# A four-layer convolution and attention kernel: residual statistics from known means, an output loop in three stages, and layer 2's statistics by sums and squares, for the last image

## The chip, the cores and the metric

The kernel runs on one core of a Trainium2 chip. The metric is the device time of one execution in microseconds (us); a kernel's time is the median of its runs. Beside those runs one execution was taken by the hardware profiler, and all lines of profile come from that one. Engines are called as in the profile: PE (TensorE, matrix products), PEld (its weight loads), DVE (VectorE), ACT (ScalarE), POOL (GpSimd) and SP (SyncE, which here only issues transfers). Each works through its own queue in order.

## The reference

Four images of 256 channels by 64 x 64 pixels, fp32. Four layers follow each other; each normalises its input by groups of 8 channels and adds its result to it.

```
x = x + L0(gn(x))   # 3x3 conv, group norm, relu -> xs; attention over the 4096 pixels; 0.1 * group_norm(w . y) + xs
x = x + L1(gn(x))   # linear attention: qkv of the rms-normed input, softmaxes, context, w_out, rms norm
x = x + L2(gn(x))   # a 3x3 depth-wise filter and a 256x256 point-wise one, both generated from the pooled input
x = x + L3(gn(x))   # one 256x256 matrix, mixed from four by a gate on the pooled input
```

`gn(x)` needs the mean and the variance of every channel of the layer's input. So between two layers lies a point where all pixels of an image must have been written and counted before the next layer can begin.

## The kernel before, in words

An image is held as two halves of 128 channels (`h`), each 128 partitions by 4096 pixels. Line 1448 on is the order of the whole: the convolution of image 0, its projections, and then, for each image, its attention (`attend`, line 887) side by side with everything else there is to do: the tail (layers 0's residual, 1, 2 and 3) of the image before and the convolution of the image after. `run` (line 1424) takes one step of a `Chain` and one step of the attention by turns. A step of the attention is eight matmul instructions of 512 columns on PE (logits, L895, and the product with the values, L934), two exponentials on ACT (L896) and one sum on DVE. All engines' queues are filled in this written order; nothing reorders them later. A `Chain` (line 45) turns the yields of its layers into steps: a yield of 0.6 at rate 1 is 0.6 of a step. `later(n, f)` emits `f` after n steps.

The last image has no attention of a next image to run beside its tail. Its tail (`tail` with `diag`, `xs_in` and `held`, line 1387) therefore runs alone at the end, with these differences:

- Layer 3's products of the image before it are held back (`held`, 16 pieces, line 1371): `fill(n)` emits n of them as work for PE at places where PE would wait, and `settle()` emits the additions on DVE and the output transfers on SP that belong to them.
- `nonlocal_out` (line 948) is layer 0's residual: for each of eight parts of 1024 columns, `big = wy * sc + xs` on DVE (through `stt`, L127), then two `bn_stats` of 512 columns each (L984). `group_finish` (line 330) joins such statistics with `bn_aggr`, averages over a group by a small matmul, and takes the inverse root with POOL. For the last image `xs` is `x_cols`, loaded into the core before its tail begins.
- `linear_attention` (line 990) ends in an output loop over eight units of 512 pixels: `outputs` (L1092 products, L1094 Squares with accumulator on ACT, then maximum on DVE and inverse root on POOL), `scaled` (the products times that root, two of four blocks on ACT at L1105 and two in one DVE operation), and `added` for the unit before (transposes on PE at L1115, addition on DVE, `bn_stats` at L1117).
- `generated` (line 1139) is layer 2: a pooled hidden layer (L1169), normalised input into `xp`, the filter `dk`, then eight parts of 1024 columns. Five of these take their taps on DVE (`taps`, eight `stt` each, L127, from ACT's `centre`, L1211), three on PE with diagonal matrices (`taps_by_products`, L1254, copied out by ACT at L1257). The point-wise matrix `pk` is summed on DVE from eight slices (`load_wp2`, loaded by SP). `pointwise` (L1219) multiplies, and `pointwise_added` adds to `big` and counts with `bn_stats` (L1228).
- `mixed` (line 1304) is layer 3: gate, a weighted sum of four matrices on DVE (L1334 and L127), scaled for each half (L1343), a bias from a small product (L1348), then 16 products (L1357), each with an addition and an output transfer.

PSUM has eight banks of 512 columns, given out in turn by `bank`; `k4` and `k2` are pools of nine tiles of 1024 and five tiles of 512 columns.

Of the kernel before, what the change touches and what calls it, by code (L numbers as in the profile page):

```python
# [13 lines left out]
P = 128  # L14
NH = 2
# [78 lines left out]
def conv_preact_fast(ctx: ExitStack, tc: tile.TileContext, guard, x, wc, wtpg, ww, wqkv, wout, w1cat, wd2,  # L94
# [235 lines left out]
    def group_finish(st, avg, eps, shift=None):  # L330


        mv = sp.tile([P, NH, 2], F32, name="mv")
        for h in range(NH):
            nc.vector.bn_aggr(mv[:, h, :], st[:, h, :, :].rearrange("p c s -> p (c s)"))
# [614 lines left out]


    def nonlocal_out(w, b, big, k4, xs_in):
# [19 lines left out]
        _, gm, rstd = yield from group_finish(wy_stats[b], avg32, 1e-5, bias)  # L972
        sc, sh = affine(gm, rstd, vec_s[:, V_G2W, :], vec_s[:, V_G2B, :], bias, 0.1)
        st = stats_tile()
        w.fill(2)
        for i, (c, h) in enumerate(PARTS):
# [6 lines left out]
            for s in range(2):  # L983
                nc.vector.bn_stats(st[:, h, 2 * c + s, :], big[:, h, bass.ts(2 * c + s, 512)])  # L984
# [5 lines left out]
    def linear_attention(w, b, big, qT, k4, st, sh, alone):  # L990
# [95 lines left out]
        def outputs(c):  # L1086
            zr = sp.tile([P, 4], F32, name="zr", bufs=3)
            banks = []
            for s in range(2):
# [5 lines left out]
                banks.append(ps)  # L1095
            nc.vector.tensor_scalar(zr, zr, 1e-24, None, ALU.max)
            rsqrt(zr, zr)
            return zr, banks

        def scaled(zr, banks):  # L1100
            z = k4("z").rearrange("p (j o) -> p j o", j=4)
            for s in range(2):
                if alone and s == 0:
                    for j in range(2):
                        nc.scalar.activation(z[:, j, :], banks[0][:, j, :], AF.Copy, scale=zr[:, j:j + 1])  # L1105
                    continue
                tt(z[:, bass.ts(s, 2), :], banks[s], zr[:, bass.ts(s, 2)].unsqueeze(2).to_broadcast([P, 2, NH * P]), ALU.mult)
            return z

        def added(c, z):  # L1110
            cols = bass.ts(c, 512)
            for h in range(NH):
# [5 lines left out]

        last = None
        for c in range(NC):  # L1120
            zb = outputs(c)
            yield 0.6
# [9 lines left out]
        w.fill(2)  # L1132
# [5 lines left out]
    def generated(w, b, big, k4, st, sh, diag):  # L1138
        _, gm, rstd = yield from group_finish(st, avg8, 1e-5, sh)
# [4 lines left out]
        w1n = sp.tile([P, NH, HP], F32, name="w1n")  # L1144
# [58 lines left out]
        st = stats_tile()  # L1203
# [20 lines left out]
        def pointwise_added(c, res):  # L1224
            cols = bass.ts(c, 512)
            for oh in range(NH):
                tt(big[:, oh, cols], res[oh], big[:, oh, cols], ALU.add)
                nc.vector.bn_stats(st[:, oh, c, :], big[:, oh, cols])  # L1228
# [36 lines left out]
        w.settle()  # L1265
# [4 lines left out]
        for n, i in enumerate(mine):  # L1270
# [9 lines left out]
            if n == 0:  # L1280
                for j in range(R):
# [19 lines left out]
    def mixed(w, b, big, k4, st, sh, held):  # L1301
# [29 lines left out]
        wm = k2("wm")  # L1331
        for j in range(NE):
            if j == 0:
                nc.vector.tensor_scalar(wm, ex[j // 2][:, j % 2, :], al[:, 0:1], None, ALU.mult)  # L1334
            else:
                stt(wm, ex[j // 2][:, j % 2, :], al[:, j:j + 1], wm, ALU.mult, ALU.add)
            yield 0.5

        mix = wm.rearrange("p (h o) -> p h o", h=NH)
        wm = []  # L1340
        for h in range(NH):
            wm.append(mix[:, h, :] if held is None else filter_tile("wmh")[:, 0, :])
            nc.vector.tensor_scalar(wm[h], mix[:, h, :], rstd[:, h:h + 1], None, ALU.mult)  # L1343
        yield 1
        pb3 = bank("ps_b3")
        for oh in range(NH):
            for h in range(NH):
                nc.tensor.matmul(pb3[:, oh:oh + 1], wm[h][:, bass.ts(oh, P)], off[:, h:h + 1],  # L1348
                                 start=(h == 0), stop=(h == NH - 1))
        b3 = sp.tile([P, NH], F32, name="b3")  # L1350
        tt(b3, sh, pb3[:, 0:NH], ALU.subtract)

        def product(c, oh):
            cols = bass.ts(c, 512)
            ps = bank("ps_ex")
            for h in range(NH):
                nc.tensor.matmul(ps, wm[h][:, bass.ts(oh, P)], big[:, h, cols], start=(h == 0), stop=(h == NH - 1))  # L1357

            def added():
                res = k2("res")  # L1360
# [3 lines left out]

        w.settle()
        for c in range(N // 512):
            for oh in range(NH):
# [659 lines left out]
```

## Time and profile before

| | |
|---|---|
| runs | 3123.15, 3116.27, 3117.10 us; median 3117.1 |
| the profiled execution: its own time, its span | 3122.35, 3120.6 us |
| busy PE, DVE, ACT, POOL | 3005.0, 2129.1, 1138.5, 131.1 us of the span |
| attention, 1024 exponentials of 128x512 on ACT (L896) | 603.7 us, 597 ns each |
| attention, 2048 + 2048 matmul instructions (L895, L934) | 968.8 and 962.1 us |
| the last eight matmul instructions of the last attention start | 2813.1 us |
| last image's tail: residual from | 2829 us |
| its layer 1: first product, first product of the output loop | 2855.4, 2922.7 us |
| its layer 2: first product of the hidden layer, first point-wise product | 2973.4, 3004.4 us |
| its layer 3: first product | 3085.6 us |

How to read it: a line of a timeline is start, duration, engine, line, operation, the tiles written and read, shapes, and how often; in brackets the idle time of the engine before it and what ended that. A line of the chain is start, duration and what the end waited for in that stretch. Matmuls overlap, so the duration of one (592 ns for 512 columns) is longer than the distance between two of them (430 ns). A matmul in fp32 appears as two instructions.

### The profile page before, as it was taken

The numbers are of one execution on the slowest core, as the hardware profiler recorded it, in microseconds if no ns is written. First come the engines' busy times: TensorE is split into PE (matmuls) and PEld (weight loads), VectorE is DVE, ScalarE is ACT, GpSimd is POOL, SyncE is SP. The second block draws the span as 40 slices with busy tenths as digits, with TensorE's granted clock in tenths as the row PEclk, the third lists the DMA queues.
The fourth block names the chain that finished last, engine by engine and source line by source line (L and its number), as shares of the span: only waits on it lengthen the run. The fifth ranks groups of instructions, "written<-read, shape, count | busy, mean of one in ns | idle before, by whom it ended". The sixth has DMA issues, their size and how long they took to land.

```text
span 3120.6 us, 24280 instructions
## 1 busy us (share of the span) xinstructions
PE 3005.0 (96%) x8606; PEld 1487.8 (48%) x8606; DVE 2129.1 (68%) x2700; ACT 1138.5 (36%) x2100; POOL 131.1 (4%) x178
## 2 busy tenths in 40 slices
PE   6899999999999999999999999999999999996888
PEld 3354555445554444444565444444555544443533
DVE  8747777853557986786537896878353768855485
ACT  2134333353545332223454432322355453333510
POOL 0100000000110000000001000000000100000100
PEclk9999999999999999999999999999999999998999
DMA  5233111032001023113200102310510010120011
GB/s 217 80 101 136 37 48 35 26 59 88 33 11 34 7 74 125 41 44 81 88 11 1 41 29 86 104 41 24 128 48 1 11 41 7 47 74 34 14 61 65
DMA packets 58912, 174.25 MB, mean 56 GB/s; under 512 B 6432, under 2 KB 16416, under 8 KB 54560
## 3 DMA queue, kind: packets, MB, share of 16 engines
q1 hardware_dynamic: 54752, 155.85, 14.5%
q0 software_dynamic: 4032, 16.78, 2.9%
q8 instruction: 70, 1.15, 0.1%
q14 instruction: 58, 0.48, 0.0%
HBM read 111.26 MB, written 78.12 MB: 61 GB/s over the span
## 4 chain that ended last, share of the span: by engine, by line
PE 76%; DVE 17%; issue 5%; ACT 1%; POOL 0%; DMA 0%; POOLq 0%; ACTq 0%; DVEq 0%
PE pf L895 22%; PE py L934 22%; PE ps_qkv L1024 5%; PE ps_conv L496 4%; DVE dw L127 4%; PE ps_tp L871 4%; PE ps_ex L1357 3%; DVE tot L124 3%; PE ps_pw L1219 3%; PE ps_conv L568 2%; PE ps_g L876 2%; PE ps_wy L918 1%; PE ps_o L1092 1%; DVE big L127 1%; PE ps_ctx L1046 1%
## 5 line engine op out<-in xcount | busy, mean ns | idle before, releaser
L896 ACT ACTIVATE pr<-pf 128x512 f32<-128x512 f32 x1024 | 603.7, 597 | 1194.1 <-PE pf L895 1148.6
L895 PE MATMUL pf<-tpg 128*128 128x512 f32 x2048 | 968.8, 595 | 1.5 <-ACT pr L896 1.5
L934 PE MATMUL py<-pr,tpg 128*128 128x512 f32 x2048 | 962.1, 592 | 3.0 <-ACT pr L896 2.9
L124 DVE TENSOR_TENSOR tot<-tot,pr 128x1024 f32<-128x1024 f32 x448 | 546.4, 1220 | 182.6 <-ACT pr L896 181.3
L934 PEld LDWEIGHTS py<-pr,tpg 128*128 128x128 f32 x2048 | 388.9, 190 | 494.7 <-issue 478.3
L895 PEld LDWEIGHTS pf<-tpg 128*128 128x128 f32 x2048 | 382.0, 190 | 436.1 <-issue 411.4
L127 DVE SCALAR_TENSOR_TENSOR dw<-xp,dk,dw 128x1008 f32<-128x1008 f32 x216 | 273.0, 1268 | 6.8 <-ACT dw L1211 3.7
L496 PE MATMUL ps_conv<-v,u 128*128 128x512 f32 x384 | 170.8, 592 | 0.0
L1024 PE MATMUL ps_qkv<-wqkv_s,xg 128*128 128x384 f32 x384 | 129.9, 487 | 0.0
L124 DVE TENSOR_TENSOR tpg<-ps_g,bg_s 128x512 f32<-128x512 f32 x32 | 22.1, 692 | 145.6 <-PE ps_g L876 145.6
L871 PE MATMUL ps_tp<-big,wtpg_s 128*128 128x512 f32 x256 | 118.1, 605 | 3.0 <-ACT big L668 3.0
L496 PEld LDWEIGHTS ps_conv<-v,u 128*128 128x128 f32 x384 | 72.8, 190 | 92.2 <-issue 91.2
L217 POOL TENSOR_TENSOR rstd<-rstd,half 128x2 f32<-128x2 f32 x24 | 16.8, 700 | 2375.5 <-DVE rstd L351 2181.1
L1219 PE MATMUL ps_pw<-dw,pk 128*128 128x512 f32 x224 | 104.6, 601 | 8.1 <-DVE dw L127 8.1
L909 DVE RECIPROCAL inv<-pss 128x512 f32<-128x512 f32 x32 | 107.3, 3352 | 7.1 <-PE pss L907 7.1
L1024 PEld LDWEIGHTS ps_qkv<-wqkv_s,xg 128*128 128x128 f32 x384 | 72.2, 190 | 53.6 <-issue 9.3
L1034 DVE TENSOR_REDUCE qs<-qk 128x16 f32<-128x512 f32 x24 | 16.5, 686 | 118.6 <-ACT qk L1028 118.6
L872 ACT ACTIVATE tpg<-ps_tp,btp_s 128x512 f32<-128x512 f32 x64 | 43.8, 687 | 119.6 <-PE ps_tp L871 119.6
L871 PEld LDWEIGHTS ps_tp<-big,wtpg_s 128*128 128x128 f32 x256 | 47.9, 195 | 55.0 <-issue 50.6
L1094 ACT ACTIVATE junk<-ps_o 128x256 f32<-128x256 f32 x128 | 49.2, 384 | 67.5 <-PE ps_o L1092 59.4
L1219 PEld LDWEIGHTS ps_pw<-dw,pk 128*128 128x128 f32 x224 | 43.0, 192 | 62.6 <-issue 52.0
L1028 ACT ACTIVATE qk<-ps_qkv,rinv 128x256 f32<-128x256 f32 x96 | 45.6, 475 | 72.4 <-PE ps_qkv L1024 61.6
(309 smaller groups left out, 3120.7 us busy)
## 6 DMA issues: line engine op xcount, KB each, us to landing
xp<-in_x_dram SPq DMA_DIRECT2D x16, 1024.0 KB, 6.3
wy_d<-wt SPq DMA_DIRECT2D x32, 512.0 KB, 3.0
out_dram<-res SPq DMA_DIRECT2D x64, 256.0 KB, 2.0
wy<-wy_d SPq DMA_DIRECT2D x28, 512.0 KB, 4.7
xs_d<-big POOLq DMA_DIRECT2D x24, 512.0 KB, 11.0
u<-filters SPq DMA_DIRECT2D x48, 256.0 KB, 2.5
xs<-xs_d SPq DMA_DIRECT2D x24, 512.0 KB, 5.3
u<-rows_d SPq DMA_DIRECT2D x36, 256.0 KB, 3.1
```

Source lines behind the costliest of these rows:

```text
L124: nc.vector.tensor_tensor(o, a, b, op)
L127: nc.vector.scalar_tensor_tensor(o, a, s, b, op0, op1)
L496: nc.tensor.matmul(ps[oh], u(oh, h), v[:, bass.ts(h, 512)], start=(h == 0), stop=(h == NH - 1))
L568: nc.tensor.matmul(ps[:, bass.ts(oh, IY * IX)], u[i][:, h, bass.ts(oh, P)], v[:, i, bass.ts(h, IY * IX)], start=(h == 0), stop=(h == NH - 1))
L871: nc.tensor.matmul(ps, wtpg_s[:, h, k, :], big[:, h, cols], start=(h == 0), stop=(h == NH - 1))
L895: nc.tensor.matmul(pf, phi[:, bass.ts(2 * m + s, P)], theta[:, bass.ts(q, 512)], start=True, stop=True)
L896: nc.scalar.activation(pr[:, bass.ts(s, 512)], pf, AF.Exp)
L909: nc.vector.reciprocal(inv, pss)
L934: nc.tensor.matmul(py, g[:, bass.ts(2 * m + s, P)], probs[i][:, bass.ts(s, 512)], start=(m == 0 and s == 0), stop=(m == NM - 1 and s == 1))
L1024: nc.tensor.matmul(ps[:, 0:3 * HID], xg[:, h, bass.ts(j, P)], wqkv_s[:, h, :], start=(h == 0), stop=(h == NH - 1))
L1219: nc.tensor.matmul(ps, pk[:, h * NH * P + oh * P:h * NH * P + (oh + 1) * P], dw[h][:, bass.ts(s, 512)], start=(h == 0), stop=(h == NH - 1))
L1357: nc.tensor.matmul(ps, wm[h][:, bass.ts(oh, P)], big[:, h, cols], start=(h == 0), stop=(h == NH - 1))
```

## The change

It concerns the last image's tail above all; `mixed`, the place of a `settle` and a small operation (`pivot`) in `generated` change for all images.

- Sums of the last image's `xs` are taken on ACT (Copy with accumulator, 16 times 512 columns) during the last steps of the last attention, three for each step. The mean of the residual is then known before it is written: the mean of `wy` (from the statistics that the attention has taken) times `sc`, plus the mean of `xs`. After each update of 1024 columns ACT takes the Square about this mean with an accumulator, in place of two `bn_stats` on DVE.
- The output loop of layer 1 (`alone`) emits the next unit's products ahead of the scaling of this one and the addition of the one before. The inverse root of the next unit is emitted between the two halves of the addition. Three of four blocks are scaled on ACT and one on DVE.
- In layer 2, for the last image, `big` is written with an accumulator (sum) on DVE, and ACT takes a Square about a pivot with an accumulator; `st()` makes mean and variance of them. `settle`, which stood before the taps, stands after the first part's taps.
- In layer 3 the matrices are mixed half by half with the normalisation's scale already in the gate; the first four products are emitted first half by first half, with the bias matmul between the halves.

```diff
-        mv = sp.tile([P, NH, 2], F32, name="mv")
-        for h in range(NH):
-            nc.vector.bn_aggr(mv[:, h, :], st[:, h, :, :].rearrange("p c s -> p (c s)"))
+        if callable(st):
+            mv = st()
+        else:
+            mv = sp.tile([P, NH, 2], F32, name="mv")
+            for h in range(NH):
+                nc.vector.bn_aggr(mv[:, h, :], st[:, h, :, :].rearrange("p c s -> p (c s)"))
...
+    res_sum = cp.tile([P, NH], F32, name="res_sum")
+    def residual_sums(xs_in):
+        parts = sp.tile([P, NH, N // 512], F32, name="res_parts", bufs=1)
+        for h in range(NH):
+            for c in range(N // 512):
+                nc.scalar.activation(junk(), xs_in[:, h, bass.ts(c, 512)], AF.Copy, accum_out=parts[:, h, c:c + 1])
+                yield
+        nc.vector.tensor_reduce(res_sum, parts, AX.X, ALU.add)
...
+        wmv, gm, rstd = yield from group_finish(wy_stats[b], avg32, 1e-5, bias)
         sc, sh = affine(gm, rstd, vec_s[:, V_G2W, :], vec_s[:, V_G2B, :], bias, 0.1)
         st = stats_tile()
+        if xs_in is not None:
+            mv = sp.tile([P, NH, 2], F32, name="mv_in", bufs=1)
+            centre = sp.tile([P, NH], F32, name="centre", bufs=1)
+            squares = sp.tile([P, NH, N // CH], F32, name="squares", bufs=1)
+            tt(mv[:, :, 0], wmv[:, :, 0], bias, ALU.subtract)
+            tt(mv[:, :, 0], mv[:, :, 0], sc, ALU.mult)
+            stt(mv[:, :, 0], res_sum, 1.0 / N, mv[:, :, 0], ALU.mult, ALU.add)
+            nc.vector.tensor_scalar(centre, mv[:, :, 0], -1.0, None, ALU.mult)
+            def moments():
+                nc.vector.tensor_reduce(mv[:, :, 1], squares, AX.X, ALU.add)
+                nc.vector.tensor_scalar(mv[:, :, 1], mv[:, :, 1], 1.0 / N, None, ALU.mult)
+                return mv
+            st = moments
         w.fill(2)
...
             yield 0.6
-            for s in range(2):
-                nc.vector.bn_stats(st[:, h, 2 * c + s, :], big[:, h, bass.ts(2 * c + s, 512)])
+            if xs_in is not None:
+                nc.scalar.activation(wy, big[:, h, cols], AF.Square, bias=centre[:, h:h + 1], accum_out=squares[:, h, c:c + 1])
+            else:
+                for s in range(2):
+                    nc.vector.bn_stats(st[:, h, 2 * c + s, :], big[:, h, bass.ts(2 * c + s, 512)])
             yield 0.6
         w.settle()
...
+            return zr, banks
+        def root(zr):
             nc.vector.tensor_scalar(zr, zr, 1e-24, None, ALU.max)
             rsqrt(zr, zr)
-            return zr, banks
         def scaled(zr, banks):
             z = k4("z").rearrange("p (j o) -> p j o", j=4)
+            if alone:
+                for j in range(4):
+                    src = banks[j // 2][:, j % 2, :]
+                    if j < 3:
+                        nc.scalar.activation(z[:, j, :], src, AF.Copy, scale=zr[:, j:j + 1])
+                    else:
+                        nc.vector.tensor_scalar(z[:, j, :], src, zr[:, j:j + 1], None, ALU.mult)
+                return z
...
-        def added(c, z):
+        def added(c, z, halves=range(NH)):
             cols = bass.ts(c, 512)
-            for h in range(NH):
+            for h in halves:
...
+        if alone:
+            this, last = outputs(0), None
+            root(this[0])
+            for c in range(NC):
+                after = outputs(c + 1) if c + 1 < NC else None
+                z = scaled(*this)
+                for h in range(NH):
+                    if last is not None:
+                        added(c - 1, last, (h,))
+                    if h == 0 and after is not None:
+                        root(after[0])
+                this, last = after, z
+                w.settle()
+                if c in (2, 4):
+                    w.fill(1)
+                yield 1
+            added(NC - 1, last)
+            w.fill(2)
+            return st
...
-        w.fill(2)
...
+        mv, gm, rstd = yield from group_finish(st, avg8, 1e-5, sh)
+        pivot = sp.tile([P, NH], F32, name="pivot")
+        tt(pivot, sh, mv[:, :, 0], ALU.subtract)
...
-        st = stats_tile()
+        if diag is None:
+            st = stats_tile()
+        else:
+            sums = sp.tile([P, 2, NH, N // 512], F32, name="sums", bufs=1)
+            def st():
+                both = sp.tile([P, 2, NH], F32, name="both_m", bufs=1)
+                mv = sp.tile([P, NH, 2], F32, name="mv")
+                nc.vector.tensor_reduce(both, sums, AX.X, ALU.add)
+                nc.vector.tensor_scalar(both, both, 1.0 / N, None, ALU.mult)
+                tt(pivot, pivot, both[:, 0, :], ALU.add)
+                tt(pivot, pivot, pivot, ALU.mult)
+                tt(mv[:, :, 1], both[:, 1, :], pivot, ALU.subtract)
+                nc.vector.tensor_copy(mv[:, :, 0], both[:, 0, :])
+                return mv
...
             for oh in range(NH):
-                tt(big[:, oh, cols], res[oh], big[:, oh, cols], ALU.add)
-                nc.vector.bn_stats(st[:, oh, c, :], big[:, oh, cols])
+                if diag is None:
+                    tt(big[:, oh, cols], res[oh], big[:, oh, cols], ALU.add)
+                    nc.vector.bn_stats(st[:, oh, c, :], big[:, oh, cols])
+                else:
+                    nc.vector.scalar_tensor_tensor(big[:, oh, cols], res[oh], 1.0, big[:, oh, cols], ALU.mult, ALU.add,
+                                                   accum_out=sums[:, 0, oh, c:c + 1])
+                    nc.scalar.activation(junk(), big[:, oh, cols], AF.Square, bias=pivot[:, oh:oh + 1],
+                                         accum_out=sums[:, 1, oh, c:c + 1])
...
         dw = {mine[0]: centre(mine[0])}
-        w.settle()
...
             if n == 0:
+                w.settle()
                 for j in range(R):
...
-        wm = k2("wm")
-        for j in range(NE):
-            if j == 0:
-                nc.vector.tensor_scalar(wm, ex[j // 2][:, j % 2, :], al[:, 0:1], None, ALU.mult)
-            else:
-                stt(wm, ex[j // 2][:, j % 2, :], al[:, j:j + 1], wm, ALU.mult, ALU.add)
-            yield 0.5
...
+        scales = sp.tile([P, NH, NE], F32, name="scales")
+        for h in range(NH):
+            nc.vector.tensor_scalar(scales[:, h, :], al, rstd[:, h:h + 1], None, ALU.mult)
+        mix = k2("wm").rearrange("p (h o) -> p h o", h=NH)
         wm = []
         for h in range(NH):
             wm.append(mix[:, h, :] if held is None else filter_tile("wmh")[:, 0, :])
-            nc.vector.tensor_scalar(wm[h], mix[:, h, :], rstd[:, h:h + 1], None, ALU.mult)
-        yield 1
-        pb3 = bank("ps_b3")
-        for oh in range(NH):
-            for h in range(NH):
-                nc.tensor.matmul(pb3[:, oh:oh + 1], wm[h][:, bass.ts(oh, P)], off[:, h:h + 1],
-                                 start=(h == 0), stop=(h == NH - 1))
+            for j in range(NE):
+                e = ex[j // 2].rearrange("p k (h o) -> p k h o", h=NH)[:, j % 2, h, :]
+                if j == 0:
+                    nc.vector.tensor_scalar(wm[h], e, scales[:, h, 0:1], None, ALU.mult)
+                else:
+                    stt(wm[h], e, scales[:, h, j:j + 1], wm[h], ALU.mult, ALU.add)
+                if j % 2 == 1:
+                    yield 0.6
+        yield 0.5
...
+        def bias():
+            pb3 = bank("ps_b3")
+            for oh in range(NH):
+                for h in range(NH):
+                    nc.tensor.matmul(pb3[:, oh:oh + 1], wm[h][:, bass.ts(oh, P)], off[:, h:h + 1],
+                                     start=(h == 0), stop=(h == NH - 1))
+            tt(b3, sh, pb3[:, 0:NH], ALU.subtract)
+        def multiply(ps, c, oh, h):
+            nc.tensor.matmul(ps, wm[h][:, bass.ts(oh, P)], big[:, h, bass.ts(c, 512)], start=(h == 0), stop=(h == NH - 1))
...
+        pieces = [(c, oh) for c in range(N // 512) for oh in range(NH)]
+        if held is not None:
+            bias()
+            for c, oh in pieces:
+                held.append(lambda c=c, oh=oh: lambda added=product(c, oh): added()())
+            return
...
         w.settle()
-        for c in range(N // 512):
-            for oh in range(NH):
-                if held is not None:
-                    held.append(lambda c=c, oh=oh: lambda added=product(c, oh): added()())
-                else:
-                    w.later(1, product(c, oh)())
-                    yield 0.1
+        first = [bank("ps_ex") for _ in range(4)]
+        for h in range(NH):
+            for ps, (c, oh) in zip(first, pieces):
+                multiply(ps, c, oh, h)
+            if h == 0:
+                bias()
+        for ps, (c, oh) in zip(first, pieces):
+            w.later(1, adder(ps, c, oh)())
+            yield 0.1
+        for c, oh in pieces[4:]:
+            w.later(1, product(c, oh)())
+            yield 0.1
...
+        sums = residual_sums(x_cols)
         while next(attention, False):
+            for _ in range(3):
+                next(sums, None)
+        for _ in sums:
             pass
         next(last)
```

Left out: `w1n` gets one buffer in place of two; where the loop for the other images called `outputs`, it now calls `root` right after it; `product` and `adder` are the former `product` in two parts.

## The prediction

> **What bounds the kernel now.** I read the page's chain first, then the chain in order of time for the last image, then busy time by stage, then the waits and the engines' timelines there.
>
> ```profile
> PE 76%; DVE 17%; issue 5%; ACT 1%; POOL 0%; DMA 0%; POOLq 0%; ACTq 0%; DVEq 0%
> ```
>
> TensorE (PE) sets the end for most of the span: until 2816 us the attention keeps it at 20.00 of 20 us. Only the last image's tail, 2816 to 3120, has holes. Busy time by stage (columns: length, then PE, PEld, DVE, ACT, POOL, the clock, DMA):
>
> ```profile
> 2820.00:2840.00 20.00, 7.07 (x18) 2.64 (x16) 17.40 (x35) 1.89 (x4) 0.70 (x1) 0.88 0.29 105
> 2840.00:2860.00 20.00, 5.75 (x17) 4.23 (x18) 13.09 (x26) 5.04 (x6) 0.76 (x2) 0.50 0.07 26
> 2940.00:2960.00 20.00, 15.83 (x72) 11.12 (x70) 15.15 (x28) 11.34 (x44) 4.03 (x4) 0.91 0.12 40
> 3020.00:3040.00 20.00, 20.00 (x48) 8.93 (x47) 18.74 (x20) 1.64 (x2) 0.00 (x0) 1.00 0.00 0
> 3040.00:3060.00 20.00, 20.00 (x48) 8.93 (x47) 18.94 (x22) 1.17 (x2) 0.00 (x0) 1.00 0.00 0
> ```
>
> The residual (first two rows) is VectorE's (DVE) alone, with ScalarE (ACT) idle. Layer 1's output loop (third) fills no engine. Layer 2's taps (last two) fill DVE and PE, PE without a gap. The chain in the residual, then the waits in the loop (total, times, longest):
>
> ```profile
> 2829.07 1.29 DVE tpg L127
> ...
> 2846.71 1.19 DVE tpg L127
> 2847.92 1.29 DVE st L984 x2
> 2849.21 1.31 DVE res L127 x2
> ```
>
> ```profile
> DVE zr L1096 <- ACT junk L1094: 12.3, 6, 3.3
> PEld ps_zt L1115 <- ACT z L1105: 5.9, 8, 1.8
> ACT junk L1094 <- issue: 5.1, 2, 2.6
> ```
>
> Every update of 1024 columns is followed by two statistics, 2.5 us a part. In the loop each engine waits for the one before it: a latency ring, not a full engine. Then three places of the tail, from the timelines:
>
> ```profile
> 2964.75 5.46 PE L1357 MATMUL ps_ex<-big,wmh 128*128 128x512 f32 x8
> ```
>
> ```profile
> 2985.94 0.75 DVE L127 SCALAR_TENSOR_TENSOR res<-ps_ex,b,big 128x512 f32<-128x512 f32 x1 [0.97 <-PE ps_ex L1357]
> ```
>
> ```profile
> 3013.60 2.07 PE L1219 MATMUL ps_pw<-dw,pk 128*128 128x512 f32 x2 [8.14 <-DVE dw L127]
> ```
>
> Held-back products delay the statistics' matmul (the next one, at 2970.0); held-back sums on DVE stand before the first tap; PE waits 8.14 us for the second part's taps, and from there to 3070.7 the chain is PE in one piece.
>
> **The skill.** *ScalarE: Activation LUTs*, section "What ACT_TABLE_LOAD costs": an ACTIVATE with a bias pointer takes 280 ns + 0.833 ns an element, and neighbours overlap by some 93 ns. For 1024 columns that is 1.13; the trace has 1.15 (L1211, one pointer) and 1.06 (L1002, Square, none): it agrees. Reading the accumulator is a second instruction of 0.19 (L1094). *TensorE: Matmul & The Clock Gate*, Part 1: after about 3.4 us of idling PE runs at half rate until it has been busy as long. The trace agrees: six point-wise matmuls took 5.49 us after the 8.14 us wait, eight take 3.43 later.
>
> **The change part by part.**
>
> A, the residual. Before, from the first update (2829.07) to the mean's shift (2851.06): 22.0 us. After: four small operations at 0.20 apart (as 2826.22, .41, .61), 0.8; eight updates at 1.28 (row of 128x1024), 10.2; then ACT's last Square, 1.15 + 0.19 + a semaphore, 1.4, beside the two held-back sums of 1.39 on DVE; a reduction and a scaling, 0.4. Sum 12.8, so **-9.2**. ACT's Squares (1.15 - 0.09 + 0.19 = 1.25 a part) hide behind the updates. If ACT can't overlap (1.44 a part) the gain is 8.0; with updates at 1.20, as the chain has some, 9.8. The last two parts' data, asked for at 2827 and landing after 4 to 5 us, are wanted at 2837.
>
> The new input sums run under attention: 16 Copies with accumulator at some 0.54 + 0.22 = 0.76, three a step: 2.3 beside 1.2 of exponentials in a 3.43 us step, just full. Behind them in ACT's queue stand the next exponentials, which PE wants 1.7 us later; the excess of 0.05 a step is covered. The tail before ends at 2787, and 5.4 of the 7 steps left are needed. Cost 0; 2 if not covered.
>
> B, the output loop. Before, from the weights (2922.69) to the group mean's copy (2970.36): 47.7. After: first Squares done at +3.2, the next unit's four (0.505 each) at +5.2, three scalings (0.37 apart) at +6.3, transposes: DVE begins at +7.1. Then its own work bounds: 16 adds with statistics at 1.385, 22.2; six scalings of 256 columns at 0.34, 2.0; six maxima, 0.6; two held-back sums, 1.4: 26.2, to +33.3. ACT needs 4 x 0.505 + 3 x 0.37 = 3.1 a unit against DVE's 3.25, PE 2.6. Two fills of 1.72 on PE stand before the next unit's products and cost about 0.5 each over PE's slack: +34.4. Aggregation and first group matmul: 1.4, so +35.8, **-11.9**. The moved root step is one DVE maximum (0.1, between the two adds) and GpSimd's power of 1.01, on a queue that holds nothing else here; its result is wanted one unit later, 3 us on, so it leaves the path. The third scaling goes from DVE to ACT, which is why DVE's share drops from 0.6 to 0.34. The last eight held-back matmuls start at about +30 and end at +33.7, before the statistics: their stall is gone. If fills stay at half clock as before (3.3 and 5.5 us) I get +39.2, -8.5; with no waits -13.2.
>
> C, the sums moved behind the first taps. Taps wait for the filter (2981.76) and ACT's centre (ends 2982.94): start at 2983.0 for 2986.6, -3.6. The four sums now follow the taps: 4 x 0.68 = +2.7. But SyncE (SP) queues their four output DMAs ahead of the third and fourth load of wp2 (before: all issued 2987.1 to 2988.6). Taps end 2993.3, sums 2996.0; the load is issued at 2996.4 and lands after 3.3 to 7.1, median 4.5, at 3000.9; DVE wants it after four products of 0.78, at 2999.1: +1.8. Net **+0.9** (-0.3 to +3.5). This moves PE's start at 3013.6 one for one.
>
> D, layer 2's statistics. DVE loses 16 x 0.6 us, but PE is full from 3013.6: nothing. At the end, instead of bn_stats 0.69 and aggregation 0.59: accumulator read 0.08, Square on 512 columns 0.77, six small operations 1.17: **+0.75** (0.5 to 1.1). A wait is added: ACT's Square waits for DVE's add, and behind it stand the copies of the PE-made depth-wise parts, which PE reads 2.8 us later at the tightest (3063.8 against 3067) and about 7 and more elsewhere: covered.
>
> E, weights in halves: before, four operations of 512 columns and two of 256 end on DVE at 3082.5; after, two tiny ones and eight of 256 (0.31 to 0.43) end at about the same time, the first half 1.7 earlier. But PE works on twelve held-back matmuls from 3077.9 to 3084.9 either way, and the bias matmuls (0.8) only change places: 0. With those twelve gone, the half would be worth its 1.7.
>
> The other images get the new order and a pivot operation of 0.16, which on every image lies in the 0.7 that DVE waits for GpSimd's power. PE is full there: 0, with -1 to +2 kept for four banks held at once.
>
> Sum: -9.2 - 11.9 + 0.9 + 0.75 = -19.5. The profiled execution took 3122.35 (span 3120.6 and 1.7 around it): 3102.9. It lies 5.25 over the runs' median of 3117.1, inside their spread; for the median, **3097.6**.
>
> **Rivals.**
> - *PE falls to half clock in the whole new loop.* Then PE needs 5.3 a unit and sets the pace; the loop comes to about 54 instead of 47.7: B is +7, total near -1, 3116. For: both fills ran at half clock before. Against: the other products ran full at half PE's load; now its share is 2.6 of 3.3. Chance 0.06.
> - *More comes free:* fills at full clock, no wait for wp2, the cold start at 3013 shortened: -25, 3092. For: the 3 us cold penalty there. Against: the 8 us wait stays. 0.12.
> - *The input sums come late*, after attention, since the tail before takes longer: 12 us of ACT before the last eviction: 3110. Against: 7 steps are left. 0.05.
> - *Slower:* the new Squares hold the depth-wise copies back. If each of six copies keeps PE waiting by two taps (2.6) and one window at half rate (1.7), 26 us are lost: +6.3, 3123. It decides once a copy is over 2.8 us late, every time; DVE, relieved of 10 us, should run ahead. 0.06.
>
> **Numbers.** Forecast 0.68; the remaining 0.03 within noise. A measurement of this kernel can tell about 0.2%, 6.2 us, from no change. Faster: 0.68 + 0.12 and half of the late sums, 0.83; same 0.11; slower 0.06. The unknown costs' bounds give 3093 to 3108; with the runs' spread 3090 to 3109.
>
> **What would show it.** Right: updates 1.28 apart in the residual and Squares beside them on ACT; 3.3 to 3.5 us a unit in the loop; the first tap 1.3 us after the filter; a wait of DVE for wp2; PE in one piece after its first point-wise matmul; the twelve held-back matmuls still ahead of the last products. Wrong: PE gaps in the taps, half clock in the loop, attention steps over 3.43 us near its end.

## The result and the profile after

The kernel after takes 3114.51 us (median of 20 runs, 3113.49 to 3116.23) against 3119.19 for the kernel before in the same sets (20 runs): a ratio of 0.9982 [0.9976, 0.9988], 4.7 us less where 19.5 were forecast. A second set on one chip gave 3114.24 (21 runs) against 3119.99 (36 runs), 0.9978 [0.9972, 0.9985]. The runs of before lie in two groups, near 3117 and near 3123, and its profiled execution (3122.35) belongs to the upper one; so the two profiles differ by 8.8 us of span (3120.6 and 3111.8), which is what the stages below add up to, and the medians by less. The later experiments are compared with 3114.24; the profile of that second set is called the second profile of after.

The stages of the two profiles, from marks in their timelines (us; the first mark of before is 2812.89 there, not 2813.1 as in the table ahead of the prediction):

| stage | before | after | difference | forecast |
|---|---|---|---|---|
| start of the span to the start of the last attention's last eight products | 2812.89 | 2816.68 | +3.8 | 0 |
| to the copy of the group mean behind the residual (A) | 39.01 | 29.07 | -9.9 | -9.2 |
| to the group mean behind layer 1 (its attention and B) | 118.46 | 114.62 | -3.8 | -11.9 |
| to PE's first point-wise product on taps made by DVE (C) | 43.24 | 47.13 | +3.9 | +0.9 |
| to the end of the last point-wise product (D's stretch) | 57.13 | 54.10 | -3.0 | 0 |
| to the group mean behind layer 2 (D's end) | 2.76 | 3.41 | +0.65 | +0.75 |
| to the end (E) | 47.1 | 46.8 | -0.3 | 0 |

The page's chain has the same shares as before, so it can't tell where the time went; it is a view of the whole span, and the tail is a tenth of it:

```profile
PE 76%; DVE 17%; issue 5%; ACT 1%; DMA 0%; POOL 0%; POOLq 0%; SPq 0%; DVEq 0%; ACTq 0%
```

Busy time by stage (length, then PE, PEld, DVE, ACT, POOL, the clock as the share of PE's full rate that was granted, DMA share and GB/s):

```profile
2820.00:2840.00 20.00, 13.98 (x27) 5.63 (x25) 16.06 (x32) 6.89 (x13) 0.70 (x1) 0.83 0.30 105
2840.00:2860.00 20.00, 11.84 (x34) 7.79 (x34) 7.52 (x18) 12.19 (x21) 1.76 (x3) 0.57 0.07 27
2920.00:2940.00 20.00, 17.41 (x77) 11.30 (x76) 11.32 (x23) 15.11 (x57) 5.04 (x5) 1.00 0.00 1
3020.00:3040.00 20.00, 20.00 (x48) 8.93 (x47) 16.35 (x20) 5.03 (x12) 0.00 (x0) 1.00 0.00 0
3040.00:3060.00 20.00, 20.00 (x48) 8.93 (x47) 11.38 (x19) 6.06 (x14) 0.00 (x0) 1.00 0.00 0
```

In the residual (first two rows) ACT now works beside DVE. In the output loop (third row) the clock is full, so PE did not fall to half rate there. DVE is busy for only 11.3 of 20 us, so it does not set the pace, as the forecast had said it would. In layer 2 (last rows) DVE is relieved and PE is as full as before.

**The residual** went as forecast. Its chain, and one pair of instructions of ACT from the timeline:

```profile
2834.89 8.45 DVE tpg L127 x7
...
2843.34 1.32 DVE res L127 x2
```

```profile
2843.37 1.15 ACT L1014 ACTIVATE wy<-tpg,centre 128x1024 f32<-128x1024 f32 x1
2844.43 0.19 ACT L1014 ACTIVATION_READ_ACCUMULATOR wy<-tpg,centre 128x1 f32 x1
```

Seven updates follow each other every 1.2 us with nothing between, and the last Square (1.15 + 0.19) ends 2.6 us after the last update began.

**The output loop** has a new ring. The timeline of one unit, cut to its links:

```profile
2933.00 1.01 POOL L217 TENSOR_TENSOR zr<-zr,half 128x4 f32<-128x4 f32 x1 [3.45 <-DVE zr L1132]
...
2934.04 1.20 ACT L1141 ACTIVATE z<-ps_o,zr 128x256 f32<-128x256 f32 x3 [1.36 <-POOL zr L217]
...
2935.35 0.48 DVE L1143 TENSOR_SCALAR z<-ps_o,zr 128x256 f32<-128x256 f32 x1 [1.14 <-ACT z L1141]
...
2935.75 0.74 DVE L127 SCALAR_TENSOR_TENSOR tpg<-ps_zt,gains,tpg 128x512 f32<-128x512 f32 x1
...
2936.53 0.69 DVE L1156 BATCH_NORM_STATS2 st<-tpg 128x6 f32<-128x512 f32 x1
...
2937.14 0.15 DVE L1132 TENSOR_SCALAR zr<-zr 128x4 f32<-128x4 f32 x1
...
2937.46 1.01 POOL L217 TENSOR_TENSOR zr<-zr,half 128x4 f32<-128x4 f32 x1 [3.45 <-DVE zr L1132]
```

Read the starts: POOL's root (1.04), ACT's three scalings (1.31), DVE's scaling (0.40), the addition (0.78), its statistics (0.61), the maximum (0.32), and POOL again: 4.46 us. The line to look at is the third: DVE scales block 4, which POOL's root has made ready at 2934.01, but begins only when ACT has finished blocks 1 to 3. It reads another part of `ps_o` and writes another part of `z`; what it shares with ACT is the PSUM bank of blocks 3 and 4. The semaphores in the trace say that this instruction waits for ACT and POOL; DVE's scaling in the kernel before, of a bank of its own, waited for POOL alone.

**Upstream**, in the other images, PE waits where it had not (total, times, longest), and the timeline shows the place:

```profile
PE ps_conv L499 <- DVE v L124: 3.6, 2, 1.8
```

```profile
1252.04 3.70 PE L499 MATMUL ps_conv<-v,u 128*128 128x512 f32 x8 [1.78 <-DVE v L124]
```

**The wait for wp2** is there, and longer than forecast:

```profile
2993.99 3.11 DVE L127 SCALAR_TENSOR_TENSOR pk<-wp,pb,pk 128x512 f32<-128x512 f32 x4 [3.29 <-DMA wp<-in_wp_dram]
```

```profile
2985.73 2.31 SPq L1450 DMA_DIRECT2D out_dram<-res  x4
2988.13 0.91 SPq L1223 DMA_DIRECT2D wp<-in_wp_dram  x2
```

SP issued the four output transfers first; the load went out at 2988.13 and landed 5.77 us later, after which DVE could go on.

### The profile page after: what moved, and what is told of

It reads as the page before. It is cut to its first block, busy times and chain, and to the rows that moved or that the text cites. A ratio compares the mean times of both kernels' runs of the same rounds, so it can differ in the third digit from the quotient of the medians.

```text
span 3111.8 us, 24418 instructions
## 1 busy us (share of the span) xinstructions
PE 3006.8 (97%) x8606; PEld 1486.8 (48%) x8606; DVE 2109.5 (68%) x2713; ACT 1174.0 (38%) x2188; POOL 131.1 (4%) x178
## 3 DMA queue, kind: packets, MB, share of 16 engines
q8 instruction: 70, 1.15, 0.2%
## 4 chain that ended last, share of the span: by engine, by line
PE 76%; DVE 17%; issue 5%; ACT 1%; DMA 0%; POOL 0%; POOLq 0%; SPq 0%; DVEq 0%; ACTq 0%
PE pf L898 22%; PE py L937 22%; PE ps_qkv L1057 5%; PE ps_conv L499 4%; DVE dw L127 4%; PE ps_tp L874 4%; PE ps_ex L1444 3%; DVE tot L124 3%; PE ps_pw L1298 3%; PE ps_conv L571 2%; PE ps_g L879 2%; PE ps_wy L921 2%; PE ps_o L1125 1%; DVE big L127 1%; DVE ra L127 1%
## 5 line engine op out<-in xcount | busy, mean ns | idle before, releaser
L217 POOL TENSOR_TENSOR rstd<-rstd,half 128x2 f32<-128x2 f32 x24 | 16.8, 701 | 2370.2 <-DVE rstd L354 2238.0
L1057 PEld LDWEIGHTS ps_qkv<-wqkv_s,xg 128*128 128x128 f32 x384 | 72.2, 190 | 53.6 <-issue 9.3
L875 ACT ACTIVATE tpg<-ps_tp,btp_s 128x512 f32<-128x512 f32 x64 | 43.7, 686 | 118.5 <-PE ps_tp L874 118.5
L874 PEld LDWEIGHTS ps_tp<-big,wtpg_s 128*128 128x128 f32 x256 | 47.5, 193 | 54.3 <-issue 49.8
```

What stands on the lines that cost most here:

```text
L874: nc.tensor.matmul(ps, wtpg_s[:, h, k, :], big[:, h, cols], start=(h == 0), stop=(h == NH - 1))
L1057: nc.tensor.matmul(ps[:, 0:3 * HID], xg[:, h, bass.ts(j, P)], wqkv_s[:, h, :], start=(h == 0), stop=(h == NH - 1))
```

## The experiments

My theory after reading the traces: four places make up the missing time. The loop has a ring closed by a shared bank; the sum of the yields in `mixed` moved the convolution against its data; the load of wp2 is late behind the outputs; and the stretch of layer 2 hangs on the remainder of the yields. The rivals name other causes for each place.

### The kernel before once more

> The kernel before, unchanged, profiled once more. The profile shown of it (span 3120.6 us) belongs to the slower half of its runs, which fall into two groups, near 3117 and near 3123. If this profile falls into the other group, the theory that the 6 us between the groups is one place (PE's clock in a stage, or a phase of the attention) expects one stage to differ by 6 us and the others by under 0.3 us. The rival, a spread over the whole span, expects every image to differ by about 1.5 us.

Measured: 3123.78, span 3122.2. It is again near 3123, so where the 6 us lie stays open. From the residual to the group mean behind layer 2 it agrees with the first profile to 0.05 us; 0.5 us more lie ahead of that and 1.1 behind.

### The scaling with a bank for each engine

```diff
-            if alone:
-                for j in range(4):
-                    src = banks[j // 2][:, j % 2, :]
-                    if j < 3:
-                        nc.scalar.activation(z[:, j, :], src, AF.Copy, scale=zr[:, j:j + 1])
-                    else:
-                        nc.vector.tensor_scalar(z[:, j, :], src, zr[:, j:j + 1], None, ALU.mult)
-                return z
             for s in range(2):
+                if alone and s == 0:
+                    for j in range(2):
+                        nc.scalar.activation(z[:, j, :], banks[0][:, j, :], AF.Copy, scale=zr[:, j:j + 1])
+                    continue
                 tt(z[:, bass.ts(s, 2), :], banks[s], zr[:, bass.ts(s, 2)].unsqueeze(2).to_broadcast([P, 2, NH * P]), ALU.mult)
```

> The kernel after, with the scaling shared out as before in layer 1's output loop: ScalarE scales both blocks of the first PSUM bank, VectorE both of the second. Theory: VectorE's scaling of block 4 waited for ScalarE's three copies because both read one bank, and that closed a ring of 4.46 us a unit. Without it VectorE scales beside ScalarE, the unit takes about 3.5 us, the loop loses 6 x 1.0 = 6 us: about 3108.5 against 3114.5. Rival: the bank is not the cause; GpSimd's power and the weights of z make the ring, and the third copy was only moved: the unit stays near 4.4 and the time within 1 us of after.

Measured: 3107.34 (5 runs), 6.9 less than after. From the third on, POOL's roots are 3.42 to 3.50 apart (4.08 and 4.09 in the two units that also take a held-back sum), and from the first root to the group mean it takes 32.3 us instead of 39.9.

### Two and two: the banks crossed, and the same operations with the banks apart

Crossed, each engine has one block of each bank; apart, ACT has the first bank and DVE the second.

```diff
-                    if j < 3:
+                    if j in (0, 2):
```

```diff
-                    if j < 3:
+                    if j < 2:
```

> The kernel after, with two scalings on each engine but crossed: ScalarE takes the first block of each PSUM bank, VectorE the second block of each (0.48 us each, same operations as in the next run). Theory (two engines on one bank wait for one another): VectorE's scalings again wait for ScalarE's, in both banks, the unit stays at 4.4 us or more: 3114 to 3116. Rival (what helped was the share of two and two, ScalarE's lighter queue): as the next run, about 3108.

> The kernel after, with two scalings on each engine and a bank for each: ScalarE the blocks of the first bank, VectorE those of the second, each block an operation of its own (2 x 0.48 us on VectorE instead of one of 0.69). Theory (the bank): no wait, a unit of about 3.7 us, 3108 to 3109. Rival (the form of VectorE's operation did it in the run with banks apart): as after, 3114.

Measured: 3111.35 crossed (6 runs) and 3106.81 apart (5 runs). Both have the same operations; from the first root to the group mean they take 37.5 and 33.7 us. One unit of each, crossed first:

```profile
2932.06 1.01 POOL L217 TENSOR_TENSOR zr<-zr,half 128x4 f32<-128x4 f32 x1 [3.04 <-DVE zr L1132]
2933.10 0.84 ACT L1141 ACTIVATE z<-ps_o,zr 128x256 f32<-128x256 f32 x2 [0.80 <-POOL zr L217]
2933.60 0.88 DVE L1143 TENSOR_SCALAR z<-ps_o,zr 128x256 f32<-128x256 f32 x2 [0.34 <-ACT z L1141]
...
2936.11 1.01 POOL L217 TENSOR_TENSOR zr<-zr,half 128x4 f32<-128x4 f32 x1 [3.04 <-DVE zr L1132]
```

```profile
2930.68 1.01 POOL L217 TENSOR_TENSOR zr<-zr,half 128x4 f32<-128x4 f32 x1 [2.67 <-DVE zr L1132]
2931.83 0.86 DVE L1143 TENSOR_SCALAR z<-ps_o,zr 128x256 f32<-128x256 f32 x2
2932.16 0.83 ACT L1141 ACTIVATE z<-ps_o,zr 128x256 f32<-128x256 f32 x2
2934.29 1.01 POOL L217 TENSOR_TENSOR zr<-zr,half 128x4 f32<-128x4 f32 x1 [2.60 <-DVE zr L1132]
```

Crossed, DVE's first scaling begins 0.50 us after ACT's first, while ACT still works on its second: it waits only for ACT's copy out of the same bank. The unit is 4.05 us. Apart, DVE waits for POOL alone and even begins before ACT; the unit is 3.61, although both engines still write one tile `z`. So the shared bank is the cause. (In this program a bank is one tile of PSUM, so the runs don't tell a rule by bank from a rule by tile.) The size I had expected for the crossed form (4.4 or more) was wrong: DVE waits for one copy instead of three there, so the ring is shorter, though it is still closed.

### All four blocks on ScalarE

```diff
-                    if j < 3:
+                    if j < 4:
```

> The kernel after, with all four scalings on ScalarE. No bank is shared and VectorE has 0.48 us less a unit; ScalarE has 4 x 0.51 + 4 x 0.37 = 3.5 us a unit. Theory (the bank closed the ring, not ScalarE's load): a unit of 3.6 to 3.8 us, 3108 to 3109.5, although ScalarE has more to do than after. Rival (ScalarE's three copies behind its Squares are the ring): longer than 4.46 by the fourth copy, 4.8 us a unit, 3117.

Measured: 3109.01 (5 runs, 3105.23 to 3109.57), 5.2 less than after, with more work on ACT. From the third on, the roots are 3.42 to 3.49 apart (one 4.12), and it takes 31.3 us from the first to the group mean. So ACT's load is not what made the ring. The profiled execution lost 1.8 us again between the group mean and the first product on taps (48.5 against 46.7 in the second profile of after), where its hidden layer took 8.2 us.

### A tenth back in the mixing stage

```diff
-        yield 0.5
+        yield 0.6
         b3 = sp.tile
```

> The kernel after, with the last weight of the stage that mixes (0.5) set to 0.6, so that a unit's weights sum to 3.0 again as before. No work changes. Theory: the sum of 2.9 moved the convolution's first product one attention step ahead of its data, and PE waited there in the images 1 and 2, 4.6 us in all; with 3.0 the two images return to 741.0 us each and the time falls by 4.6 to about 3110. Rival: what the new order asks of other images (four banks at once, a pivot on VectorE) costs the 4.6: no change, 3114.5.

Measured: 3106.84 (5 runs), 7.4 less than after. PE has no wait for `v` at `ps_conv` any more, and the last attention's last products start at 2811.65 instead of 2816.68, 5.0 earlier. The new order of layer 3, with its four banks at once, is still there: it costs other images nothing. Of the 7.4, 5.0 are seen in that place against the first profile of after and 6.3 against the second (2817.99). The profiled execution is the slowest of its five (1.1 over the median); what is left stays unplaced.

### The sums after all eight slices, and ahead of the taps

```diff
-                w.settle()
                 for j in range(R):
...
+                w.settle()
```

> The kernel after, with the held-back sums (and their output DMAs) moved from behind the first four slices of the point-wise weights to behind all eight, so that SyncE issues every load of these weights ahead of the output DMAs. Theory: VectorE's wait of 3.3 us for the third load goes, and PE's first point-wise product comes 3.3 us earlier: about 3111.2. Rival: the load is late because the transfers themselves are slow (5.8 us for 512 KB wherever it is issued), or the sums themselves set PE's start: under 1 us.

Measured: 3111.71 (6 runs), 2.5 less than after. DVE goes through all eight slices without a wait, and then the sums:

```profile
2986.12 6.26 DVE L127 SCALAR_TENSOR_TENSOR pk<-wp,pb,pk 128x512 f32<-128x512 f32 x8
2992.29 2.72 DVE L127 SCALAR_TENSOR_TENSOR res<-ps_ex,b,big 128x512 f32<-128x512 f32 x4
```

```diff
         dw = {mine[0]: centre(mine[0])}
+        w.settle()
...
-                w.settle()
```

> The kernel after, with the four held-back sums back ahead of the first taps, as before: part C undone. Theory: the first tap comes 3.6 us later, but the 2.7 us of sums and the 3.3 us of waiting for the third load go from behind the taps: 2.4 us less, 3112; and PE's stretch from the first point-wise product is 57 us again if it was C that let two depth-wise products run ahead of it (then 3115), 54 if not. Rival: C is worth what it was meant for: 1 to 3 us more than after, 3116 to 3118.

Measured: 3113.61 (11 runs), 0.6 less than after. From the group mean to PE's first product on taps it is 44.8 us instead of 46.7 in the second profile of after, but the stretch behind it is 55.2 instead of 54.7. Both sides of the expectation missed in part: moving the sums cost 1.9 us in its own place, and in all 0.6, little more than the 0.3 by which the two sets of after differ. What remains over before (44.8 against 43.2) is the hidden layer, below.

### Layer 2's statistics as before

```diff
-                if diag is None:
+                if True:
                     tt(big[:, oh, cols], res[oh], big[:, oh, cols], ALU.add)
                     nc.vector.bn_stats(st[:, oh, c, :], big[:, oh, cols])
```

(and likewise where `st` is made.)

> The kernel after, with layer 2's statistics as before (VectorE adds and takes the statistics of each part), part D undone. Theory: PE is full there, so VectorE's relief is worth nothing, and the 3 us by which PE's stretch of taps got shorter came from the order of the work ahead of it; undoing D gives back 0.6 us at the end: 3113.9. Rival: the relief let VectorE run ahead and made the stretch 3 us shorter: 3117.0, and the stretch is back at 57.1 us.

Measured: 3114.22 (15 runs), no difference. The stretch is 54.3 us, the end 2.70 instead of 3.40; the 0.6 less that this made one expect doesn't show in the median. DVE's relief is worth nothing, and it is not what made the stretch 3 us shorter.

### The remainder of the yields: put back, and taken from the kernel before

```diff
-            added(NC - 1, last)
+            yield 0.6; added(NC - 1, last)
```

```diff
             yield 0.6
-        yield 1
+        yield 0.4 if alone else 1
         added(NC - 1, last)
```

> The kernel after, with one more weight of 0.6 behind the last unit of layer 1's output loop, so that the remainder of its weights is 0.6 as before. No work changes; the point-wise products of layer 2 come one tap earlier into PE's queue. Theory (the remainder made the stretch of layer 2 shorter): the stretch from the first point-wise product to the last is 57 us again, 3 us more, 3117. Rival (parts C and D did it together): 54 to 55 us and 3114.

> The kernel before, with the last weight of layer 1's output loop 0.4 instead of 1, so that the remainder of 0.6 is gone. Theory: the stretch of layer 2 takes 54 to 55 us instead of 57.1, and the time falls by 2 to 3 us (0.999 of before). Rival: it needs the moved sums or the new statistics too: 57 us and no change.

Measured: 3117.22 for after with the 0.6 (21 runs), 3.0 more than after; 3121.24 for before without it (13 runs) against 3122.13, a ratio of 0.9998 [0.9990, 1.0006]. In the stretch: 56.2 us with the remainder on the new kernel, 55.4 without it on the old one (57.1 with). The diagonal products on PE ahead of the first point-wise product, of after and of after with the 0.6:

```profile
2977.38 20.55 PE L1339 MATMUL ps_dw<-xp,tpg 128*128 128x512 f32 x48
```

```profile
2978.99 18.86 PE L1339 MATMUL ps_dw<-xp,tpg 128*128 128x512 f32 x44
```

Four more matmul instructions (1.7 us) lie in the time in which PE waits for DVE anyway. In the new kernel the remainder is the main cause: putting it back lengthened the stretch by 1.5 to 2.1 us (from 54.7 and 54.1), not quite to the 57 that was expected. The median rose by more, and in the profiles the twenty matmuls behind layer 2 (held-back ones and the first products) took 11.3 us instead of the 10.3 and 10.7 of after. On the old kernel, taking it away shortened the stretch by 1.7 us, but the time didn't follow: 1.0 us came back behind layer 2, where twelve held-back matmuls took 8.1 instead of 7.0.

### The residual alone on the kernel before

```diff
+        wmv, gm, rstd = yield from group_finish(wy_stats[b], avg32, 1e-5, bias)
...
+            if xs_in is not None:
+                nc.scalar.activation(wy, big[:, h, cols], AF.Square, bias=centre[:, h:h + 1], accum_out=squares[:, h, c:c + 1])
...
+        sums = residual_sums(x_cols)
         while next(attention, False):
+            for _ in range(3):
+                next(sums, None)
```

> The kernel before with part A alone: the known mean, the Squares on ScalarE and the sums of the input under attention. Theory: 9.9 us less in the tail and nothing elsewhere, so 0.9968 of before (about 3109.3 if before is at 3119.2). Rival: the sums of the input or ScalarE's new work disturb attention or the evictions ahead of the tail: under 8 us, with the difference in the images 1 to 3.

Measured: 3109.07 (6 runs), 0.9966 [0.9954, 0.9978] of before. The residual takes 28.9 us instead of 39.0, and the last attention ends where it did (2812.91 against 2812.89): the sums of the input under attention are free. "Nothing elsewhere" missed: layer 1, where nothing was edited, took 115.0 us instead of 118.5 in these profiles, with a granted clock of 0.92 instead of 0.90. The median with this one part is lower than that with the whole change.

### The mended kernel, and it with the old statistics

Three edits at once (banks apart, 0.6 in the mixing stage, sums behind all slices), then also the old statistics of layer 2.

> The kernel after, unchanged, beside the others of this set on one chip, so that their differences don't contain that of two chips. Expected: 3114.5 within 1.5 us. If it comes out near 3112 here, the gains of the single experiments against 3114.5 were overstated by as much.

> The kernel after with three edits at once: the scaling shared out as before (a bank for each engine), the last weight of the mixing stage 0.6, and the sums behind all eight slices of the point-wise weights. Theory: they lie in three different places and add up: 7.0 + 5.0 + 2.8 = 14.8 us less than after, about 3099.7. Rival: one of them is hidden by another, or the runs drift from set to set: 3103 or more.

> The kernel with three edits mended (banks apart, weight 0.6 in the mixing stage, sums behind all slices) and layer 2's statistics as before. Theory: VectorE's relief is worth nothing here and the accumulated sums cost 0.65 us at the end: 3097.2 against 3097.9. Rival: with the earlier start of the taps VectorE's relief pays now, and without it the time is over 3099.

Measured: 3114.24 for after, 3097.90 (5 runs, 0.9928 [0.9914, 0.9941] of before) for the three edits: 16.3 less than after, where the single ones gave 6.9, 7.4 and 2.5, 16.8 in all. They add up. With the old statistics 3093.75 (5 runs, 3093.18 to 3098.58, 0.9916 [0.9903, 0.9930]). Of the 4.1 us between the two profiles' spans only 0.7 is the statistics (the end 2.70 instead of 3.41); 2.2 lie in layer 1 ahead of the loop (granted clock from 2840 to 2855: 0.73 against 0.60) and 1.7 in the hidden layer (5.4 instead of 7.1 us), neither of which the edit touches. What the edit itself is worth is 0.7 at the end, as expected; the rest of the 4.1 is not shown to be its doing.

## Why the prediction was wrong

**A was right** (-9.2, measured -9.9): the updates came at 1.20 apart, the end of the range that the forecast had named at 9.8, and the input sums cost 0.

**B failed at the step "Then its own work bounds".** The sum took each engine's load for a unit (DVE 3.25, ACT 3.1, PE 2.6 us) and let the three scalings of ACT and the one of DVE run side by side. They can't as the program is built: blocks 3 and 4 share a bank, DVE's scaling waits for ACT's last one, and the unit was 4.46 us. From the first product to the group mean's copy, the marks of the forecast, the loop took 47.7 us before and 43.4 after: -4.3, so 7.6 us of the -11.9 were missing. DVE's first addition came 9.9 us after the first product instead of 7.1; the rest went unit by unit. With banks apart it came after 7.1, DVE's instructions followed each other without a gap, 3.43 us a unit, and the loop took 35.8 us, the forecast's figure. So DVE was the bound there, as forecast; that the figure fits to 0.1 us is in part luck, since DVE scaled two blocks in that run (0.59 us) where the sum had one (0.34).

The Trainium skill describes such a wait, in *PSUM — Partial Sum Buffer*, section "PSUM bank collisions raise a hardware error": the compiler's scheduler "adds a dependency between any two instructions on different engines that touch the same bank × 32-partition quadrant, reads and writes alike". The runs agree as far as the wait goes (0.31 to 1.14 us a wait from the third unit on, gone with banks apart). Which step of the build put the wait into this program is not shown, and no run tried the two reads without it. The forecast had priced the operations and not asked what the split needs of the bank. The stall of the last eight held-back matmuls did go.

**"The other images ... 0" failed.** The forecast had looked for added work and kept up to 2 us for four banks at once. The work was free; the yields were not. A sum of 2.9 in `mixed` where there had been 3.0 put the convolution's first product one attention step ahead of its data, twice: +3.8.

**C was right in kind and wrong in two terms.** The wait for wp2 was foreseen, with a landing after 4.5 us and 1.8 of wait; it landed after 5.8 and DVE waited 3.3. The range for the landing went up to 7.1, but its middle was too low for this load: in the profile of before the third and fourth load of wp2 had taken 6.3 and 7.1 us. The other term was not there at all: PE's hidden layer took 7.0 us instead of 5.4, because the clock was lower. The hidden layer before, then after (columns as above, the clock is the third number from the end):

```profile
2973.25:2978.61 5.36, 5.36 (x45) 1.83 (x42) 5.11 (x9) 2.57 (x5) 0.00 (x0) 1.00 0.26 98
```

```profile
2963.20:2970.25 7.05, 7.05 (x45) 2.24 (x42) 5.81 (x9) 2.58 (x5) 0.00 (x0) 0.76 0.52 162
```

The 17 profiles divide without an exception. Where the last held-back matmuls end 0.15 or 0.16 us ahead of the group mean's copy, so that PE goes from them straight to the statistics, the hidden layer takes 5.4 us at a granted clock of 1.00 (the four of the old loop and two of the new). Where PE has been idle between (they end 0.5 to 1.4 us ahead, eleven profiles), it takes 6.8 to 8.2 us at 0.65 to 0.78. The stall that B took away had kept PE busy up to the statistics. The forecast quoted the Trainium skill, *TensorE: Matmul & The Clock Gate*, Part 1, for the six point-wise products, and didn't apply it here. As quoted, with 3.4 us of idling, it would not have foretold this: in the profile of after PE's gaps here are 0.7, 0.8 and 1.5 us, with matmuls of 0.3 to 0.4 us between them. No run changed this gap alone, so it is a reading of the traces, and 1.7 us is its size.

**D.** Its end was right (+0.65 against +0.75), and so was the worth of DVE's relief (0). But "PE in one piece" was taken for a fixed length. The stretch is as long as what is left for it, and 1.7 to 3.0 us of it moved ahead, into PE's wait for the taps, since the loop's yields sum to 8.0 and not 10.6.

**E was right**, 0 within 0.3. Of the rivals, half clock in the whole loop fell, although its 3116 lies nearer to the measured time than the forecast does: the granted clock was 1.00 from 2920 to 2940 and 0.83 from 2940 to 2960. Late input sums fell (2812.91 for the last eight products with part A alone), and so did Squares that hold the copies back (PE is full, 20.00 of 20). "More comes free" was right only in that the stretch got shorter. The sum: 7.6 (the bank) + 3.8 (the yields upstream) + 3.0 (C) - 3.0 (the stretch) - 0.7 (A) = 10.7 us, which is what lies between the forecast 19.5 and the 8.8 between the profiles. The other 4.1 of the miss lie between profiles and medians: the profiled execution of before was 3.2 over its median, and that of after 0.8 under its own (0.1 is between times and spans).

## What to carry to other kernels

When a step is shared out between two engines, ask first which PSUM bank each half reads, and follow the ring from one unit's root to the next before adding up loads: an engine that is busy 57% of the time can be in it. In a program whose order is written by counted steps, a change of a tenth in a weight is a change like any other: compare the order of the queues, in the parts that were not meant to change too. Try the parts of a change alone; here one part was worth more than all five.

## What was unexpected on the chip

- DVE scales a 128x256 block out of PSUM in 0.48 us and two of them in 0.86 to 0.88 together, while one operation over 128x512 with a tensor of scales takes 0.67 to 0.69: two small operations took longer than one for the same columns.
- An execution's stages move by 2 us without any edit: from the residual's group mean to the first root it was 74.7 and 72.2 us in two profiles of the same kernel. The clock granted from 2845 to 2860, at its beginning, was 0.59 and 0.72. In this stage a difference under 2.5 us between two profiles proves nothing. Other stages kept closer: C took 47.1 and 46.7 us, the stretch 54.1 and 54.7. Medians and repeated marks (periods, waits) carry the argument.
- The third and fourth load of wp2, 512 KB each, took 5.8 and 6.5 us to land in one profile of after and 5.3 and 6.1 in the other; the forecast's middle had been 4.5.
